# Rolling 28 of 32 batch tiles of a pairwise-product kernel into a staged hardware loop

## The chip, the cores and the metric

The kernel runs on one core of a Trainium2 chip. The metric is the device time of one execution in microseconds (us).

## The reference, cut to what matters

```python
# inputs: x (4096, 32, 64) float32, W (496, 64, 64) float32
i_idx, j_idx = np.triu_indices(32, k=1)            # 496 pairs i < j
vdotw = jnp.einsum('bpd,pde->bpe', x[:, i_idx, :], W)
return (vdotw * x[:, j_idx, :]).reshape(4096, -1)  # (4096, 31744)
```

Each row has 32 fields of 64 numbers. For every pair of fields, the first is multiplied by a matrix of that pair and the product, element by element, by the second field. The output has 520 MB, against 42 MB of input and weights that are read.

## The kernel before

The 4096 rows are cut into 32 batch tiles of 128 rows. The weights stay in SBUF. For each tile the kernel loads x (1 MB, issued by ScalarE's queue), transposes it with TensorE (PE in the profile), multiplies it with the weights of two fields at a time into one of four PSUM slots, and VectorE (DVE) multiplies the slot with x into a slice of a ring in SBUF. Five stores per tile, of 7552, 6528, 5504, 6336 and 5824 columns, carry the slices to the output. SyncE (SP in the profile) issues them. Engines wait for each other and for transfers: in the profile of this kernel SyncE waits 159 times for DVE before a store, and DVE 53 times for a store to land. All 32 tiles are unrolled.

```python
STORES = [[0, 1], [2, 3], [4, 5], [6, 7, 8], [9, 10, 11, 12, 13, 14, 15]]
RING = 28160
...
xpool  = ctx.enter_context(tc.tile_pool(name="x", bufs=2))
xtpool = ctx.enter_context(tc.tile_pool(name="xT", bufs=2))
psum   = ctx.enter_context(tc.tile_pool(name="ps", bufs=4, space=bass.MemoryType.PSUM))
...
ring = const.tile([P, RING], F32, tag="ring", name="ring")
...
for t in range(NT):                                   # 32 tiles, unrolled
    xt, xT = xs.pop(t), xTs.pop(t)
    if t + 1 < NT:
        xs[t + 1] = load_x(t + 1)                     # next x, one tile ahead
    for s, group in enumerate(STORES):
        if at + store_w[s] > RING:
            at = 0
        osb = ring[:, at : at + store_w[s]]
        at += store_w[s]
        for p in group:
            ...                                       # transposes of the next tile
            nc.tensor.matmul(pm[...], xT[...], w_sb[p][...])
            nc.vector.tensor_tensor(osb[...], pm[...], xt[...], ALU.mult)
        nc.sync.dma_start(out=out[ts(t, P), o0 : o0 + store_w[s]], in_=osb)
```

Of the kernel before, what the change touches and what calls it, by code (L numbers as in the profile page):

```python
# [1 line left out]

# [6 lines left out]

F32 = mybir.dt.float32  # L10
ALU = mybir.AluOpType

P = 128
BANK = 512

STORES = [[0, 1], [2, 3], [4, 5], [6, 7, 8], [9, 10, 11, 12, 13, 14, 15]]
PREFETCH_AT = [5, 6]
RING = 28160


@with_exitstack
def pair_bilinear_kernel(
    ctx: ExitStack,
    tc: tile.TileContext,
    x: bass.AP,
    w: bass.AP,
    out: bass.AP,
    F: int,
    D: int,
):  # L30
















    nc = tc.nc
    B = x.shape[0]
    NT = B // P
    NPR = F // 2  # L50

    width = [(F - 1 - i) * D for i in range(F)]
    off = [sum(width[:i]) for i in range(F)]
    woff = [sum(width[0 : 2 * p : 2]) for p in range(NPR)]
    store_w = [sum(width[2 * p] + width[2 * p + 1] for p in g) for g in STORES]

    const = ctx.enter_context(tc.tile_pool(name="const", bufs=1))
    xpool = ctx.enter_context(tc.tile_pool(name="x", bufs=2))
    xtpool = ctx.enter_context(tc.tile_pool(name="xT", bufs=2))
    psum = ctx.enter_context(tc.tile_pool(name="ps", bufs=4, space=bass.MemoryType.PSUM))  # L60

    ident = const.tile([P, P], F32, tag="ident", name="ident")
    make_identity(nc, ident)

    def runs(tl, a, b, n):

        ap = tl[:, a : a + n]
        return bass.AP(ap.tensor, ap.offset, [list(ap.ap[0]), [b - a, 2], list(ap.ap[1])])

    def load_x(t):  # L70
        xt = xpool.tile([P, F * D], F32, tag="x", name=f"x_{t}")
        nc.scalar.dma_start(out=xt, in_=x[ts(t, P), :])
        return xt

    def transpose_x(xT, t, xt, g):

        n = 2 * BANK // P
        pt = psum.tile([P, 2 * BANK], F32, tag="ps", name=f"pt_{t}_{g}")
        for c in range(n):
            nc.tensor.transpose(pt[:, ts(c, P)], xt[:, ts(n * g + c, P)], ident)  # L80
        nc.scalar.copy(xT[:, ts(g, 2 * BANK)], pt)  # L81

    def new_xT(t):
        return xtpool.tile([P, NPR * P], F32, tag="xT", name=f"xT_{t}")

    ring = const.tile([P, RING], F32, tag="ring", name="ring")
    at = 0
    xs = {0: load_x(0)}

    w_sb = []  # L90
    for p in range(NPR):
        wp = const.tile([P, width[2 * p]], F32, tag=f"w{p}", name=f"w{p}")
        nc.sync.dma_start(out=wp, in_=w[:, woff[p] : woff[p] + width[2 * p]])
        w_sb.append(wp)

    xTs = {0: new_xT(0)}
    for g in range(2):
        transpose_x(xTs[0], 0, xs[0], g)

    for t in range(NT):  # L100
        xt, xT = xs.pop(t), xTs.pop(t)
        if t + 1 < NT:
            xs[t + 1] = load_x(t + 1)
        for s, group in enumerate(STORES):
            if at + store_w[s] > RING:
                at = 0
            osb = ring[:, at : at + store_w[s]]
            at += store_w[s]
            o0 = off[2 * group[0]]
            for p in group:  # L110
                if t + 1 < NT and p in PREFETCH_AT:
                    if t + 1 not in xTs:
                        xTs[t + 1] = new_xT(t + 1)
                    transpose_x(xTs[t + 1], t + 1, xs[t + 1], PREFETCH_AT.index(p))
                for c0 in range(0, width[2 * p], BANK):
                    pm = psum.tile([P, 2, BANK], F32, tag="ps", name=f"pm_{t}_{p}_{c0}")
                    n = [max(0, min(BANK, width[2 * p + h] - c0)) for h in range(2)]
                    for h in range(2):
                        if n[h]:
                            nc.tensor.matmul(  # L120
                                pm[:, h, : n[h]],
                                xT[h * D : (h + 1) * D, ts(p, P)],
                                w_sb[p][h * D : (h + 1) * D, c0 : c0 + n[h]],
                                start=True,
                                stop=True,
                            )
                    o = [off[2 * p + h] - o0 + c0 for h in range(2)]
                    xj = [(2 * p + h + 1) * D + c0 for h in range(2)]
                    if n[0] == n[1]:
                        nc.vector.tensor_tensor(  # L130
                            runs(osb, o[0], o[1], n[0]),
                            pm[:, :, : n[0]],
                            runs(xt, xj[0], xj[1], n[0]),
                            ALU.mult,
                        )
                    else:
                        for h in range(2):
                            if n[h]:
                                nc.vector.tensor_tensor(  # L139
                                    osb[:, o[h] : o[h] + n[h]],  # L140
                                    pm[:, h, : n[h]],
                                    xt[:, xj[h] : xj[h] + n[h]],
                                    ALU.mult,
                                )
            nc.sync.dma_start(out=out[ts(t, P), o0 : o0 + store_w[s]], in_=osb)


# [33 lines left out]
```

## Time and profile before

| | before |
|---|---|
| time, median of 2 runs | 1341.47 us (1341.44 to 1341.51) |
| span of the profiled run | 1339.7 us |
| mean granted TensorE clock, as a share of full speed | 0.949 |
| DVE busy, PE busy | 88%, 86% of the span |
| a store from issue to landing | 22 us |
| one batch tile in the steady state, between landings of the last stores of neighbouring tiles | 41.0 to 41.3 us, some up to 41.7 |

The prediction below shows the lines of the page and of the waits that carry the reading. A second view places one tile in the middle of the kernel: busy time of each engine in a window that is one tile long. Its columns are the window and its length, the busy time of each engine with the number of instructions, the granted clock, the busy share of the DMA engines, and what they moved.

```profile
core 0: us, PE busy (x) PEld busy (x) DVE busy (x) ACT busy (x) POOL busy (x), PEclk, DMA share, GB/s
800.00:841.00 41.00, 34.37 (x162) 15.83 (x162) 35.27 (x50) 2.02 (x2) 0.00 (x0) 0.96 0.98 412
```

In 41 us DVE is busy for 35.3 us and PE for 34.4 us, while the DMA engines are busy 98% of the time. The transfers bound the tile. The next lines of the same page are the queues that fetch instructions.

```profile
q8 instruction: 42, 0.69, 0.2%
q14 instruction: 23, 0.19, 0.0%
```

### The profile page before, as it was taken

The page shows a single profiled execution, that of the slowest core. Times are in us where ns is not written, and L with a number is a line of the kernel's source. Part 1 is how long each engine was busy: PE and PEld are TensorE (multiplying, and loading weights), DVE is VectorE, ACT ScalarE, POOL GpSimd, SP SyncE. Part 2 cuts the span into 40 slices and gives each one's busy share as a digit, 9 for nine tenths or more (in the row PEclk, how much of TensorE's full clock was granted, in tenths as well). Part 3 has the DMA queues.
Part 4 walks back from the last instruction along what each step waited for, and adds up shares of the span by engine and source line. Part 5 has one row for each costly group of instructions (what it writes and reads, how often), then busy time and mean ns, then how long its engine had stood idle before and what let it go on. Part 6 is the DMA issues. An engine that isn't in the chain of part 4 may idle for free.

```text
span 1339.7 us, 13755 instructions
## 1 busy us (share of the span) xinstructions
PE 1151.0 (86%) x5376; PEld 548.7 (41%) x5376; DVE 1177.4 (88%) x1664; ACT 66.1 (5%) x65; POOL 0.7 (0%) x6
## 2 busy tenths in 40 slices
PE   7998889888898888988888978889798897888992
PEld 3444344443343443443433534444344443444441
DVE  6999889888899988989888989899898997898993
ACT  1000000000000000000000000000000000000000
POOL 0000000000000000000000000000000000000000
PEclk9999889999999999989999899899898998998996
DMA  9999999999999999999999999999999999999996
GB/s 392 426 431 434 429 431 429 427 427 434 426 434 430 422 422 430 422 424 429 415 426 424 426 426 404 415 420 431 428 420 408 431 427 431 416 424 420 422 429 264
DMA packets 30017, 562.93 MB, mean 420 GB/s; under 512 B 3456, under 2 KB 3840, under 8 KB 5376
## 3 DMA queue, kind: packets, MB, share of 16 engines
q1 hardware_dynamic: 25344, 528.49, 92.6%
q10 hardware_dynamic: 4608, 33.56, 6.0%
q8 instruction: 42, 0.69, 0.2%
q14 instruction: 23, 0.19, 0.0%
HBM read 41.94 MB, written 520.09 MB: 420 GB/s over the span
## 4 chain that ended last, share of the span: by engine, by line
DMA 54%; DVE 23%; PE 11%; issue 9%; DVEq 0%
DMA out_dram<-ring 54%; DVE ring L130 15%; PE pm L120 9%; DVE ring L139 9%; PE pt L80 2%; DMA x<-in_x_dram 1%; DVEq L130 0%; DVEq L177 0%
## 5 line engine op out<-in xcount | busy, mean ns | idle before, releaser
L120 PE MATMUL pm<-w,xT 64*128 64x512 f32 (+7 forms) x4864 | 1083.2, 559 | 158.3 <-DVE ring L130 140.1
L130 DVE TENSOR_TENSOR ring<-pm,x 128x1024 f32<-128x1024 f32 x768 | 904.0, 1217 | 138.4 <-DMA out_dram<-ring 93.0
L120 PEld LDWEIGHTS pm<-w,xT 64*128 64x128 f32 x4864 | 487.7, 194 | 720.1 <-DVE ring L130 451.3
L139 DVE TENSOR_TENSOR ring<-pm,x 128x448 f32<-128x448 f32 (+6 forms) x896 | 330.2, 415 | 3.6 <-PE pm L120 2.9
L81 ACT COPY xT<-pt 128x1024 f32<-128x1024 f32 x64 | 64.8, 1012 | 1194.6 <-PE pt L80 1194.6
L80 PE MATMUL pt<-ident,x 128*128 128x128 f32 x512 | 76.5, 297 | 8.5 <-DMA x<-in_x_dram 8.5
L80 PEld LDWEIGHTS pt<-ident,x 128*128 128x128 f32 x512 | 61.0, 152 | 48.9 <-issue 35.3
L81 ACT ACT_TABLE_LOAD x1 | 1.3, 1283 | 1.7 <-PEq L173 1.7
masks.py:199 POOL TENSOR_SCALAR_AFFINE_SELECT ident<-ident 128x128 f32<-128x128 f32 x1 | 0.3, 292 | 0.1
masks.py:197 POOL MEMSET ident<- 128x128 f32 x1 | 0.2, 204 | 0.3 <-POOLq L173 0.3
L173 POOL MEMSET const-bfloat16-1.0<- 128x1 bf16 x1 | 0.1, 101 | 0.0
L173 POOL MEMSET const-uint8-127<- 128x1 uint8 x1 | 0.1, 101 | 0.0
L173 POOL MEMSET const-float32-0.0<- 128x1 f32 x1 | 0.1, 98 | 0.2 <-issue 0.2
L173 POOL MEMSET const-float32-1.0<- 128x1 f32 x1 | 0.1, 98 | 0.0
## 6 DMA issues: line engine op xcount, KB each, us to landing
out_dram<-ring SPq DMA_DIRECT2D x32, 3776.0 KB, 22.8
out_dram<-ring SPq DMA_DIRECT2D x32, 3264.0 KB, 21.8
out_dram<-ring SPq DMA_DIRECT2D x32, 3168.0 KB, 22.4
out_dram<-ring SPq DMA_DIRECT2D x32, 2912.0 KB, 22.3
out_dram<-ring SPq DMA_DIRECT2D x32, 2752.0 KB, 22.1
x<-in_x_dram ACTq DMA_DIRECT2D x32, 1024.0 KB, 14.2
w<-in_w_dram SPq DMA_DIRECT2D x1, 992.0 KB, 7.4
w<-in_w_dram SPq DMA_DIRECT2D x1, 928.0 KB, 11.7
```

What stands on the lines that cost most here:

```text
L80: nc.tensor.transpose(pt[:, ts(c, P)], xt[:, ts(n * g + c, P)], ident)
L81: nc.scalar.copy(xT[:, ts(g, 2 * BANK)], pt)
L120: nc.tensor.matmul(pm[:, h, : n[h]], xT[h * D : (h + 1) * D, ts(p, P)], w_sb[p][h * D : (h + 1) * D, c0 : c0 + n[h]], start=True, stop=True,)
L130: nc.vector.tensor_tensor(runs(osb, o[0], o[1], n[0]), pm[:, :, : n[0]], runs(xt, xj[0], xj[1], n[0]), ALU.mult,)
L139: nc.vector.tensor_tensor(osb[:, o[h] : o[h] + n[h]], pm[:, h, : n[h]], xt[:, xj[h] : xj[h] + n[h]], ALU.mult,)
L173: nc = bacc.Bacc("TRN2", target_bir_lowering=False, num_devices=1)
```

## The change

The intent is a smaller program: two tiles stay unrolled at the head and two at the tail, and the 28 between them become seven iterations of a hardware loop whose body holds four tiles. In place of rotating pools, x, its transpose and the PSUM slots become fixed buffers, used in the same order as before. The loop is "staggered": its body is divided into four stages, one per tile, and the semaphores of a stage are reset when the engines have left it, so that engines need not all meet at the end of an iteration. The step from the end of one iteration to the start of the next is called the back edge here. The row address of every load and store inside the loop is a register plus a constant. The ring becomes 1888 columns smaller and starts at column 0 in every iteration.

```diff
-RING = 28160
+RING = 26272
+HEAD = 2
+BODY = 4
 ...
-    xpool = ctx.enter_context(tc.tile_pool(name="x", bufs=2))
-    xtpool = ctx.enter_context(tc.tile_pool(name="xT", bufs=2))
-    psum = ctx.enter_context(tc.tile_pool(name="ps", bufs=4, ...))
+    xbuf = [const.tile([P, F * D], F32, ...) for k in range(2)]
+    xTbuf = [const.tile([P, NPR * P], F32, ...) for k in range(2)]
+    slots = [pspool.tile([P, 2, BANK], F32, ...) for k in range(4)]
 ...
-            nc.sync.dma_start(out=out[ts(t, P), o0 : o0 + store_w[s]], in_=osb)
+            nc.sync.dma_start(out=out[bass.ds(row, P), o0 : o0 + store_w[s]], in_=osb)
+
+    for t in range(HEAD):
+        batch_tile(t * P, t % 2, (t + 1) * P)
+    turn["at"] = 0
+    tail = NT - (NT - HEAD - 1) % BODY - 1
+    with tc.For_i(HEAD * P, tail * P, BODY * P, iteration_sync="staggered") as r:
+        for j in range(BODY):
+            batch_tile(r + j * P, (HEAD + j) % 2, r + (j + 1) * P)
+            if j + 1 < BODY:
+                tc.stage_boundary()
+    turn["at"] = 0
+    for t in range(tail, NT):
+        batch_tile(t * P, t % 2, (t + 1) * P if t + 1 < NT else None)
```

`batch_tile(row, k, nxt)` is the body of the old loop, with `xbuf[k]` for x and `nxt` as the row of the next load.

More of the change, by code (lines that the diff above doesn't have):

```diff
@@ L57, in pair_bilinear_kernel, with slot @@
     const = ctx.enter_context(tc.tile_pool(name="const", bufs=1))
-    xpool = ctx.enter_context(tc.tile_pool(name="x", bufs=2))
-    xtpool = ctx.enter_context(tc.tile_pool(name="xT", bufs=2))
-    psum = ctx.enter_context(tc.tile_pool(name="ps", bufs=4, space=bass.MemoryType.PSUM))
+    pspool = ctx.enter_context(tc.tile_pool(name="ps", bufs=1, space=bass.MemoryType.PSUM))
     ident = const.tile([P, P], F32, tag="ident", name="ident")
     make_identity(nc, ident)
+    ring = const.tile([P, RING], F32, tag="ring", name="ring")
+    xbuf = [const.tile([P, F * D], F32, tag=f"x{k}", name=f"x{k}") for k in range(2)]
+    xTbuf = [const.tile([P, NPR * P], F32, tag=f"xT{k}", name=f"xT{k}") for k in range(2)]
+    slots = [
+        pspool.tile([P, 2, BANK], F32, tag=f"ps{k}", name=f"ps{k}") for k in range(4)
+    ]
+    turn = {"slot": 0, "at": 0}
+    def slot():
+        turn["slot"] = (turn["slot"] + 1) % 4
+        return slots[turn["slot"]]
     def runs(tl, a, b, n):
@@ L68, in runs, with load_x, transpose_x @@
         return bass.AP(ap.tensor, ap.offset, [list(ap.ap[0]), [b - a, 2], list(ap.ap[1])])
-    def load_x(t):
-        xt = xpool.tile([P, F * D], F32, tag="x", name=f"x_{t}")
-        nc.scalar.dma_start(out=xt, in_=x[ts(t, P), :])
-        return xt
-    def transpose_x(xT, t, xt, g):
+    def load_x(row, k):
+        nc.scalar.dma_start(out=xbuf[k], in_=x[bass.ds(row, P), :])
+    def transpose_x(k, g):
         n = 2 * BANK // P
-        pt = psum.tile([P, 2 * BANK], F32, tag="ps", name=f"pt_{t}_{g}")
+        pt = slot().rearrange("p a b -> p (a b)")
         for c in range(n):
-            nc.tensor.transpose(pt[:, ts(c, P)], xt[:, ts(n * g + c, P)], ident)
-        nc.scalar.copy(xT[:, ts(g, 2 * BANK)], pt)
-    def new_xT(t):
-        return xtpool.tile([P, NPR * P], F32, tag="xT", name=f"xT_{t}")
-    ring = const.tile([P, RING], F32, tag="ring", name="ring")
-    at = 0
-    xs = {0: load_x(0)}
+            nc.tensor.transpose(pt[:, ts(c, P)], xbuf[k][:, ts(n * g + c, P)], ident)
+        nc.scalar.copy(xTbuf[k][:, ts(g, 2 * BANK)], pt)
+    load_x(0, 0)
     w_sb = []
@@ L94, in pair_bilinear_kernel, with batch_tile @@
         w_sb.append(wp)
-    xTs = {0: new_xT(0)}
     for g in range(2):
-        transpose_x(xTs[0], 0, xs[0], g)
-    for t in range(NT):
-        xt, xT = xs.pop(t), xTs.pop(t)
-        if t + 1 < NT:
-            xs[t + 1] = load_x(t + 1)
+        transpose_x(0, g)
+    def batch_tile(row, k, nxt):
+        xt, xT = xbuf[k], xTbuf[k]
+        if nxt is not None:
+            load_x(nxt, 1 - k)
         for s, group in enumerate(STORES):
-            if at + store_w[s] > RING:
-                at = 0
-            osb = ring[:, at : at + store_w[s]]
-            at += store_w[s]
+            if turn["at"] + store_w[s] > RING:
+                turn["at"] = 0
+            osb = ring[:, turn["at"] : turn["at"] + store_w[s]]
+            turn["at"] += store_w[s]
             o0 = off[2 * group[0]]
             for p in group:
-                if t + 1 < NT and p in PREFETCH_AT:
-                    if t + 1 not in xTs:
-                        xTs[t + 1] = new_xT(t + 1)
-                    transpose_x(xTs[t + 1], t + 1, xs[t + 1], PREFETCH_AT.index(p))
+                if nxt is not None and p in PREFETCH_AT:
+                    transpose_x(1 - k, PREFETCH_AT.index(p))
                 for c0 in range(0, width[2 * p], BANK):
-                    pm = psum.tile([P, 2, BANK], F32, tag="ps", name=f"pm_{t}_{p}_{c0}")
+                    pm = slot()
                     n = [max(0, min(BANK, width[2 * p + h] - c0)) for h in range(2)]
@@ L144, in pair_bilinear_kernel @@
                                 )
-            nc.sync.dma_start(out=out[ts(t, P), o0 : o0 + store_w[s]], in_=osb)
+            nc.sync.dma_start(out=out[bass.ds(row, P), o0 : o0 + store_w[s]], in_=osb)
+    for t in range(HEAD):
+        batch_tile(t * P, t % 2, (t + 1) * P)
+    turn["at"] = 0
+    first_slot = turn["slot"]
+    tail = NT - (NT - HEAD - 1) % BODY - 1
[4 more added lines that the diff above has]
+                tc.stage_boundary()
+    assert turn["slot"] == first_slot
+    turn["at"] = 0
+    for t in range(tail, NT):
+        batch_tile(t * P, t % 2, (t + 1) * P if t + 1 < NT else None)
 def kernel(r_inputs, L0_rec_W):
```

## The prediction

> **What bounds the kernel now.** I read the page first, its slices, queues and chain, then the waits of the issuing queue, then the waits of the engines. The slices show whether anything rests:
>
> ```profile
> span 1339.7 us, 13755 instructions
> PE 1151.0 (86%) x5376; PEld 548.7 (41%) x5376; DVE 1177.4 (88%) x1664; ACT 66.1 (5%) x65; POOL 0.7 (0%) x6
> ...
> DMA  9999999999999999999999999999999999999996
> GB/s 392 426 431 434 429 431 429 427 427 434 426 434 430 422 422 430 422 424 429 415 426 424 426 426 404 415 420 431 428 420 408 431 427 431 416 424 420 422 429 264
> ...
> q1 hardware_dynamic: 25344, 528.49, 92.6%
> q10 hardware_dynamic: 4608, 33.56, 6.0%
> ...
> DMA 54%; DVE 23%; PE 11%; issue 9%; DVEq 0%
> ```
>
> The transfers never rest: the DMA row is 9 in every slice but the last, and the two data queues fill 98.6% of the 16 engines' time. The stores (q1) are most of it, and the chain that ended last is 54% store. PE and DVE are at 86% and 88%, so the kernel is transfer-bound, with DVE some 4 to 5 us per batch tile behind it (1339.7 less 1177.4, over 32 tiles).
>
> Why the transfers never rest is in the list of issues and in the waits of SyncE, which issues all stores:
>
> ```profile
> out_dram<-ring SPq DMA_DIRECT2D x32, 3776.0 KB, 22.8
> out_dram<-ring SPq DMA_DIRECT2D x32, 3264.0 KB, 21.8
> ...
> SPq L145 <- DVE ring L139: 1228.7, 159, 10.5
> ...
> DVE ring L130 <- DMA out_dram<-ring: 93.0, 53, 3.3
> ```
>
> A store takes 22 us from issue to landing, though one is issued about every 8.3 us (160 stores in 1330 us): two to three are always queued. SyncE waits 159 times, every time for DVE to have filled the slice of the ring and never for a store to land. DVE in its turn waits 93 us for old stores to free the ring. So each store's start-up and acknowledgement are hidden beneath the stores queued ahead of it. That is what I look at in the change.
>
> [...] packet records show one row of the 5824-column store (23,296 bytes) taking 865 ns, or 26.9 GB/s on each of 16 engines. The first weight load's first packet starts 1.0 us after its issue on an idle queue, and the last store lands 0.45 us after its last packet. No run yet shows a store alone. [...]
>
> **The change part by part.** Arithmetic, matmuls, multiplies, loads and stores are the same in number and shape. The smaller ring keeps the reuse distance: I walked both placements, and a slice still comes back after three or four stores. The fixed PSUM slots turn in the same order as the pool. What is new are waits, and I took them from the built program, instruction by instruction.
>
> 1. *Stores one after another.* In the loop the row address of a store is a register, and the program orders stores to the output against each other. The second store of a stage waits for the semaphore that the first one raises on landing, the third for the second, and so on; a stage's first store waits for the last one of the stage before. In the kernel before a store waits for DVE and for a semaphore last used about eight transfers earlier. So inside the loop exactly one store is in flight, and its fixed cost is exposed every time.
>  Cost of a store alone: eight rows per engine at 26.9 GB/s, which is 8.97, 7.76, 6.54, 7.53 and 6.92 us for the five, 37.7 us per tile. The fixed part: 1.0 us to the first packet, 0.45 us from last packet to landing, 0.1 us to wake SyncE[...]: 1.9 us[...]. Five of them: 9.5 us. The x load of the next tile (8192-byte packets, eight per engine at 309 ns, 2.5 us) now starts at the stage's entry and shares the engines with one store: 2.5 us. [...] A loop tile costs 37.7 + 9.5 + 2.5 + 0.5 = **50.2 us**, against 41.5 before (from the landings of equal stores in neighbouring tiles).
>
> 2. *Stage gates.* An engine enters a stage only when all have left the stage two back, and SyncE says so only at its own entry, after it has issued the last store of the stage just before. So PE cannot run ahead over a boundary: it starts the next tile when that last store is issued. From there 0.4 us of waits, 1.3 us for the first matmuls and 8.5 us of DVE work (spacing of stores in the unobstructed second tile) make the next tile's first store ready after 10.2 us. The last store lands after 6.9 + 2.5 + 1.9 = 11.3 us. The gate is therefore just hidden by the serial store, and I charge nothing; 1.1 us is little slack.
>
> 3. *The back edge.* In the first stage of an iteration DVE's very first multiply, too, waits for all five stores of the iteration's end to land. The 8.5 us of DVE work then lie bare, with 0.2 us of semaphores: **8.7 us** for each of six back edges, 52 us. [...]
>
> 4. *Entry and exit.* Two head tiles run as before; their stores would land by 110.6 us after the start. DVE may finish the loop's first slice only after the last of them: the first loop store is issued near 115.5 us. The last two tiles run unserialised again. From the issue of the loop's last store I count 12 us until the next can start, two tiles of transfers (75.4 + 2.5 us) and 1.5 us for start and landing: 91 us.
>
> Sum: 115.5 + 28 x 50.2 + 52 - 11.3 (the last store's own time, counted in the tail) + 91 = 1653 us, and 1.8 us for the time over the span (1341.5 against 1339.7): **1655 us**.
>
> **Rivals.**
> - *Hidden anyway.* If the waits on landing were already met when reached, DVE being late, nothing would change: 1340 to 1360 us. Against it: DVE needs 38 us per tile unobstructed and the serial stores 47 us, so DVE is always ahead, and the wait is on the transfer just issued, which cannot have landed.
> - *Gates alone.* If I misread the store semaphores and only the stage gates counted, each boundary would cost DVE about 2 us of start-up, against 4 to 5 us of slack per tile: within 2%, with entry and exit perhaps 1365 us. For it: the list of the kernel before names the same family of semaphores, harmlessly. Against it: in the loop the store's semaphore is the one raised by its predecessor.
> - [...]
> - *Less than I count.* If the fixed cost of a store is 1.5 us, the 140 stores give back 56 us: 1600 us.
>
> **Range and chances.** The fixed cost is the term that matters: 0.1 us of it is 14 us of time. From 1.5 to 2.4 us[...] I get 1590 to 1730 us. Only the first two rivals bring it below a 2% loss (1368 us), and the built program speaks against both: slower by over 2% with 0.97, within 2% with 0.025, faster with 0.005. There is no way to be faster that I see: the bytes stay.
>
> **What would show it.** Step 1 is right if SyncE's waits move from DVE to its own stores in the loop, if a store takes 8.5 to 13 us to landing instead of 22, and if the DMA row falls to 8. Step 2 is right if the first slice of a tile is ready about when the last store lands; wrong if SyncE waits for DVE at each boundary. Step 3 is right if seven regular pauses of some 9 us stand in the transfers, about 210 us apart. DVE's and PE's busy sums should stay near 1177 and 1151 us, a longer PE sum meaning a lower clock. The prediction is wrong if stores still overlap in the loop, or if a lone store's fixed cost is outside 1.5 to 2.4 us.

The packet records are those of the kernel before. The fixed part of a store came to 1.9 us: the three terms make 1.55 us, and the rest was an allowance. The loop tile came to 50.2 us, and its 0.5 us are such an allowance too. So the 1655 us hold about 28 x (5 x 0.35 + 0.5) = 63 us that rest on no trace. A rival that put more time at the boundaries and the back edges is cut; without it the range from 1.5 to 2.4 us is 1599 to 1725 us. The small terms that stay are estimates from the profile of before: 0.1, 0.2 and 0.4 us of waking and waiting (there, DVE multiplies 0.12 us after a landing, 1278.88 to 1279.00 us), and 1.3 us for the first matmuls (1.18 us from the first matmul, at 11.98 us, to the first multiply).

## The result and the profile after

| | before | after |
|---|---|---|
| time, median of 2 runs | 1341.47 us | 1630.63 us (1630.26 to 1631.0) |
| ratio, 95% interval | | 1.2156 (1.2103 to 1.2208) |
| span, mean granted clock | 1339.7 us, 0.949 | 1629.2 us, 0.873 |
| one batch tile | 41.0 to 41.3 us | 48.9 to 49.8 us, and 56.0 to 56.3 us with a back edge |

A ratio here is the mean time of one kernel's runs over that of the other's of the same rounds, so it is not quite the ratio of the medians that are quoted. The kernel became 289 us slower. The page of the kernel after:

```profile
span 1629.2 us, 14956 instructions
PE 1175.0 (72%) x5376; PEld 558.4 (34%) x5376; DVE 1175.1 (72%) x1664; ACT 66.1 (4%) x65; POOL 0.7 (0%) x6
...
PEclk9977988789887898888988899888998889988798
DMA  9987787788887888877888778887788877888799
...
q1 hardware_dynamic: 25344, 528.49, 77.6%
q10 hardware_dynamic: 4608, 33.56, 4.9%
q8 instruction: 10, 0.16, 0.0%
q14 instruction: 7, 0.06, 0.0%
...
out_dram<-ring SPq DMA_DIRECT2D x32, 3776.0 KB, 10.3
out_dram<-ring SPq DMA_DIRECT2D x32, 3264.0 KB, 9.2
```

The work is unchanged: the same counts of matmuls and multiplies, DVE's busy sum 1175.1 us as against 1177.4, and the same number of packets on the two data queues. PE's busy sum is 1175.0 us as against 1151.0, at a mean granted clock of 0.873 as against 0.949. But no engine is close to full any more. The stores and loads fill 82.5% of the DMA engines' time instead of 98.6%, and the row of slices is 7 or 8 wherever the loop runs and 9 in the unrolled ends. A store takes 10.3 us from issue to landing where it took 22.8: nothing is queued ahead of it. The waits of SyncE name the reason; the columns are the total, the number of waits and the longest.

```profile
SPq L149 <- DMA out_dram<-ring: 1029.5, 118, 11.8
SPq L149 <- DVE ring L143: 453.2, 78, 19.0
```

Before, 159 waits of stores were for DVE and none for another store. Now 118 are for a store to land. The other 78 are for DVE (one store can have both waits); the long ones among them, as the windows and the timelines below show, are at the boundaries of tiles.

Three windows that each hold one tile of the loop, from the first store of a tile to that of the next; the first holds a back edge, and the third ends 0.7 us later than its tile (columns as before):

```profile
270.04:326.27 56.23, 37.26 (x166) 17.80 (x166) 36.58 (x53) 2.02 (x2) 0.00 (x0) 0.85 0.74 308
326.27:375.86 49.59, 37.06 (x174) 17.99 (x172) 36.91 (x53) 2.02 (x2) 0.00 (x0) 0.86 0.84 349
375.86:425.50 49.64, 36.59 (x174) 17.20 (x172) 37.40 (x53) 2.02 (x2) 0.00 (x0) 0.90 0.83 349
```

DVE still needs only 37 us of each tile. The inner tile in the second window has 49.6 us, in which DMA is busy 83 to 84%. I took one such tile apart with the packet records, in which the profile gives start and length of every DMA packet. From the landing of one store, SyncE issues the next after 0.12 us; the first packet starts 0.83 us after the issue; the 16 engines end within 0.15 us of each other; the landing is signalled 0.37 us after the last packet. That is 1.47 us in every store in which the engines move nothing. The medians from issue to landing are 10.34, 9.17, 7.92, 8.90 and 10.51 us. The fifth shares the engines with the load of x and takes 2.2 us longer than without it. The five add up to 46.8 us, four wakings of 0.12 us make it 47.3, and the rest of the 49.6 us is a gap before a tile's first store.

That gap is the second thing to see. The timeline at the boundary of two tiles (start, duration, engine, operation; idle time before it in brackets). The last store of the old tile was issued at 363.11 and landed at 373.65; the first of the new one was issued at 375.86:

```profile
363.95 12.54 PE L124 MATMUL ps<-w,xT 64*128 64x512 f32 x48 [10.95 <-issue]
364.93 0.37 PEld L124 LDWEIGHTS ps<-w,xT 64*128 64x128 f32 x2 [0.48 <-issue]
365.79 0.37 PEld L124 LDWEIGHTS ps<-w,xT 64*128 64x128 f32 x2 [0.49 <-issue]
366.17 1.22 DVE L134 TENSOR_TENSOR ring<-ps,x 128x1024 f32<-128x1024 f32 x1 [11.54 <-PE ps L124]
...
371.01 0.28 PEld L124 LDWEIGHTS ps<-w,xT 64*128 64x128 f32 x2 [0.15 <-issue]
371.44 0.28 PEld L124 LDWEIGHTS ps<-w,xT 64*128 64x128 f32 x2 [0.15 <-issue]
```

PE has been idle for 10.95 us: the stage gate holds it until SyncE has issued the old tile's last store. It then starts slowly. Its pairs of weight loads come 0.86 us apart, and from 369.1 on 0.43 us apart, twice as fast. The granted clock of these two stretches, the column after POOL, is half and full:

```profile
363.11:368.92 5.81, 4.97 (x12) 2.37 (x14) 2.30 (x2) 0.00 (x0) 0.00 (x0) 0.50 0.88 342
368.92:375.86 6.94, 6.94 (x34) 3.40 (x32) 6.64 (x10) 0.00 (x0) 0.00 (x0) 1.00 0.75 295
```

DVE starts 3.06 us after the store's issue, and its slice is ready 12.75 us after it, when the store has already been down for 2.2 us.

The third is the back edge. The last store of the iteration landed at 317.26:

```profile
317.38 3.48 DVE L134 TENSOR_TENSOR ring<-ps,x 128x1024 f32<-128x1024 f32 x3 [19.10 <-DMA out_dram<-ring]
...
326.27 0.34 SPq L149 DMA_DIRECT2D out_dram<-ring  x1
```

DVE waited for the transfers to end and then filled a whole slice while nothing moved: 9.0 us. All six back edges have it, between 8.75 and 9.02 us.

### The profile page after: what moved, and what is told of

The parts are those of the page before. It is cut to its first block, busy times and chain, and to the rows that moved or that the text cites. A ratio compares the mean times of both kernels' runs of the same rounds, so it can differ in the third digit from the quotient of the medians.

```text
span 1629.2 us, 14956 instructions
## 1 busy us (share of the span) xinstructions
PE 1175.0 (72%) x5376; PEld 558.4 (34%) x5376; DVE 1175.1 (72%) x1664; ACT 66.1 (4%) x65; POOL 0.7 (0%) x6
## 5 line engine op out<-in xcount | busy, mean ns | idle before, releaser
L124 PE MATMUL ps<-w,xT 64*128 64x512 f32 (+7 forms) x4864 | 1112.3, 574 | 429.5 <-issue 305.1
L134 DVE TENSOR_TENSOR ring<-ps,x 128x1024 f32<-128x1024 f32 x768 | 904.1, 1213 | 439.7 <-PE ps L124 307.4
L124 PEld LDWEIGHTS ps<-w,xT 64*128 64x128 f32 x4864 | 502.0, 199 | 1012.7 <-issue 523.0
L143 DVE TENSOR_TENSOR ring<-ps,x 128x448 f32<-128x448 f32 (+6 forms) x896 | 327.5, 411 | 0.0
L92 ACT COPY xT<-ps 128x1024 f32<-128x1024 f32 x64 | 64.8, 1012 | 1495.9 <-PE ps L91 1495.9
L91 PE MATMUL ps<-ident,x 128*128 128x128 f32 x512 | 71.4, 284 | 8.6 <-DMA x<-in_x_dram 8.6
L91 PEld LDWEIGHTS ps<-ident,x 128*128 128x128 f32 x512 | 56.4, 143 | 42.0 <-issue 42.0
## 6 DMA issues: line engine op xcount, KB each, us to landing
out_dram<-ring SPq DMA_DIRECT2D x32, 3776.0 KB, 10.3
out_dram<-ring SPq DMA_DIRECT2D x32, 2912.0 KB, 10.5
```

The source lines that it names most:

```text
L91: nc.tensor.transpose(pt[:, ts(c, P)], xbuf[k][:, ts(n * g + c, P)], ident)
L92: nc.scalar.copy(xTbuf[k][:, ts(g, 2 * BANK)], pt)
L124: nc.tensor.matmul(pm[:, h, : n[h]], xT[h * D : (h + 1) * D, ts(p, P)], w_sb[p][h * D : (h + 1) * D, c0 : c0 + n[h]], start=True, stop=True,)
L134: nc.vector.tensor_tensor(runs(osb, o[0], o[1], n[0]), pm[:, :, : n[0]], runs(xt, xj[0], xj[1], n[0]), ALU.mult,)
L143: nc.vector.tensor_tensor(osb[:, o[h] : o[h] + n[h]], pm[:, h, : n[h]], xt[:, xj[h] : xj[h] + n[h]], ALU.mult,)
```

## The experiments

The theory has three parts: stores that wait for their predecessor (**order**), stage gates that start a tile too late (**gates**), and a multiply that waits for a whole stage of stores (**back edge**). The rivals are that one of them alone carries the time, or that the loop itself (branches, fetches, registers) costs it. All kernels below gave the reference's result. The kernel before ran beside each group with medians of 1341.21, 1341.44 and 1341.24 us.

### e4_serial: the order alone, without a loop

The kernel before, unrolled, with one wait added from each store to the previous one.

```diff
-            nc.sync.dma_start(out=out[ts(t, P), o0 : o0 + store_w[s]], in_=osb)
+            st = nc.sync.dma_start(out=out[ts(t, P), o0 : o0 + store_w[s]], in_=osb)
+            if last:
+                tc.add_manual_dep(st.ins, last.pop().ins.name, SYNC, reason="one store at a time")
+            last.append(st)
```

> The unrolled kernel of before with one thing added: each store waits until the store before it has landed; no loop, no stages, no branch. Theory (store order): a tile costs what a tile of the changed kernel costs without its stage gap, 49.6 - 2.2 = 47.4 us, so 24.5 us until the first store, 32 x 47.4 us, and 1.8 us: 1543 us, range 1525 to 1560. Rival (the loop's machinery, that is gates, semaphore resets, branch and instruction fetch, costs most): nothing of it is here, so about 1341 us, at most 1400.

Measured: **1621.75 us** (2 runs), ratio 1.2092 (1.2049 to 1.2135). The waits and the slices:

```profile
SPq L147 <- DMA out_dram<-ring: 1524.7, 159, 13.6
...
DMA  9888888888888889888887888878888888878888
```

Order alone, with no loop, no gate and no back edge, costs 280 us. That confirms the mechanism, but it is 79 us more than I expected, so the expectation missed. The packet records point to a reason. This unrolled program fetches instructions in 65 packets, as before does. Of 140 stores in tiles 2 to 29, 55 had a fetch in flight, and these took 1.0 to 1.4 us longer on average than the same store without one (the first of a tile 11.35 us against 10.35). That is some 66 us, if the fetch is what makes the difference. In the kernel before the 65 fetch packets lie under queued stores, which take 22 us from issue to landing. e10_serial_loop below repeats the serial stores without the fetches.

### e1_nodep: the order taken away, the loop kept

```diff
+            st = nc.sync.dma_start(out=out[bass.ds(row, P), o0 : o0 + store_w[s]], in_=osb)
+            tc.add_to_no_dep_group("stores", st.ins)
+            tc.declare_no_dep(st.ins, group="stores", reason="rows and columns are disjoint")
```

> The changed kernel with the stores declared independent of each other inside an iteration; gates, resets, back edge and branch stay. Theory: the serial part goes, the 6 back edges (DVE still waits for the last store of an iteration) cost some 10 us of idle transfers each and the entry 5 us, the gates take about 3 us of DVE time per boundary, which its slack of some 3 us nearly covers: 1410 us, range 1375 to 1445. Rival (loop machinery): hardly less than 1630, at least 1550.

Measured: **1408.46 us** (2 runs), ratio 1.0502 (1.0471 to 1.0532).

```profile
SPq L149 <- DVE ring L143: 1161.6, 159, 19.1
SPq L149 <- DMA out_dram<-ring: 93.9, 12, 8.7
...
DMA  9998999879998899978999789997999969999998
```

Three quarters of the loss are gone (222 of 289 us), SyncE waits for DVE again, and the DMA row is 9 but for a dip at every fifth slice. Inner tiles take 41.3 us, as before, with the gates still there. The tiles after a back edge take 50.9 us, 9.8 us more; six of them and 5.6 us at the entry of the loop make 64 of the 67 us that remain over before. So the loop as such costs nothing in an inner tile, and the gates cost nothing while stores are queued.

### e2_early: the gates opened earlier, the order kept

Each engine announces that it has left the previous stage after the second store of its tile instead of at its entry to the next stage.

```diff
+            if early and s == 1:
+                for e in LEAVE:                 # SP, DVE, PE, Activation
+                    tc.previous_stage_wait(e)
```

> The changed kernel with SyncE, DVE, PE and ScalarE signing out of the stage before already after the second store of a stage, so that PE may cross the next boundary without waiting for the last store to be issued; stores still one after another. Theory: the gap before a tile's first store falls from 2.2 us (1.2 to 2.4) to 0.1 us at 21 inner boundaries, 44 us in all; the back edge keeps its 9 us: 1587 us, range 1575 to 1600. Rival (loop machinery is most of the 289 us): below 1450.

Measured: **1596.39 us** (2 runs), ratio 1.1903 (1.1868 to 1.1938), 34.2 us less than after.

```profile
SPq L151 <- DMA out_dram<-ring: 1232.7, 139, 11.3
SPq L151 <- DVE ring L145: 208.8, 45, 19.0
```

The gap before a tile's first store is 0.02 us at all 21 inner boundaries and still 8.76 to 9.02 us at the six back edges. SyncE's waits for DVE fall from 453 to 209 us. 34.2 us over 21 boundaries is 1.6 us each, a little less than the gaps that vanished (most of them 1.7 to 2.4 us). The load of x is issued at another point and now mostly shares the engines with the third store instead of the fifth. By the stores' times to landing it costs 2.7 us a tile on average there, against 2.2 to 2.3 us in the kernel after. That is some 13 us over the loop, and it accounts for the 10 us between the 44 us of gaps that vanished and the 34 us that were won.

### e7_halves: the back edge, by two rings

The ring becomes two buffers of 14080 columns with two stores in each, so that the first multiply of an iteration meets a buffer whose last store is the third of the stage before, not the fifth.

```diff
-RING = 26272
+RING = 14080
-    ring = const.tile([P, RING], F32, tag="ring", name="ring")
+    ring = [const.tile([P, RING], F32, tag=f"ring{k}", name=f"ring{k}") for k in range(2)]
...
+            at = turn["at"] if turn["n"] % 2 else 0
+            osb = ring[turn["n"] // 2 % 2][:, at : at + store_w[s]]
+            turn["n"], turn["at"] = turn["n"] + 1, at + store_w[s]
```

> The changed kernel with the ring made of two buffers of 14080 columns, two stores in each, so that DVE's first multiply of an iteration waits only for the stores of its own half, which landed long before. Reuse distance 4 everywhere. Theory: the gap at the 6 back edges falls from 9.0 us to the 2.3 us of an inner boundary, 40 us: 1590 us, range 1578 to 1605. Rival (the back edge gap is the branch and its instruction fetch): 1630 us, unchanged.

Measured: **1584.14 us** (2 runs), ratio 1.1812 (1.1777 to 1.1846), 46.5 us less than after. The gap at a back edge falls from 9.0 us to between 1.7 and 2.15 us, which is the gap of the inner boundaries. Six times 6.9 us is 41 us. The rest is the same wait at the loop's entry, where the ring's restart makes DVE wait for the head's stores: the first store of the second loop tile is issued at 160.2 us instead of 167.0. The end of the kernel gives 1.7 us of it back. The slices lose their regular sevens:

```profile
DMA  9998787888888888888888888888888888888799
```

Since the branch is still there and the gap at a back edge is now like that at an inner boundary, no cost of the branch is left to be seen.

### e8_nodep_early: order and gates removed

The edits of e1 and e2 together.

> The changed kernel with the stores declared independent and the early signing-out together; only the back edge is left. In the run with independent stores alone the inner tiles already took 41.3 us against 41.1 before and those at the back edge 50.9. Theory: early signing-out gives at most 0.2 us at 21 boundaries, and the 6 back edges keep 9.8 us each: 1404 us, range 1390 to 1412. Rival (the gates hold back the transfers although the inner tiles look untouched): under 1380.

Measured: **1409.06 us** (4 runs), ratio 1.0506 (1.0488 to 1.0523). It is the time of e1. Inner tiles take 40.8 to 41.4 us and those after a back edge 51.2 to 51.5. Opening the gates is worth 34 us when stores are serial and nothing when they are queued.

### e9_all: all three removed

The edits of e1, e2 and e7.

> The changed kernel with all three: independent stores, early signing-out, and the ring in two halves so that DVE does not wait for the last store at the back edge. SyncE still waits there for the last store to land. Theory: 6 back edges x 1.5 us of fixed cost are all that is left, 1341 + 9 = 1350 us,[...] 1343 us, range 1325 to 1360. Rival (a loop costs something more that these three do not cover): above 1370.

Measured: **1355.01 us** (4 runs), ratio 1.0100 (1.0083 to 1.0117).

```profile
DMA  9999999989999899999999899998999989999998
...
SPq L150 <- DVE ring L144: 975.5, 141, 12.2
SPq L150 <- DMA out_dram<-ring: 126.2, 18, 9.8
```

This accounts for all but 13.5 us of the 289. Inner tiles take 41.1 to 41.3 us, as before. The six tiles after a back edge take 42.7 us, 1.5 us more: there SyncE still waits for a landing, and the fixed cost of one store lies bare. That is 9 us. Of the other 4 us, 1 us lies outside the profiled span (2.9 us of time over the span instead of 1.8), and the rest is spread over head and inner tiles. I had expected 1343 us, 12 us too low though inside the range given: 1350 us with the wait at the back edge, less 7 us from a term that no run had shown. The loop's fewer fetches (17 packets instead of 65) give nothing back where stores are queued.

### c1_before_halves: the two rings without a loop

A control: the kernel before with the two half rings of e7.

> Control: the unrolled kernel of before with its ring made of the same two halves; no loop. If a gain of the run with all three came from the ring, it is here too. Theory: the same capacity, so 1341 us, range 1334 to 1347.

Measured: **1341.76 us** (4 runs), ratio 1.0002 (0.9986 to 1.0019). The half rings are neutral on their own, so what they win in e7 and e9 is the wait at the back edge.

### e5_barrier: no stages, a barrier at each iteration's end

```diff
-    with tc.For_i(HEAD * P, tail * P, BODY * P, iteration_sync="staggered") as r:
+    with tc.For_i(HEAD * P, tail * P, BODY * P, iteration_sync="barrier") as r:
...
-            if j + 1 < BODY:
-                tc.stage_boundary()
```

> The changed kernel with the loop's semaphores reset at a full barrier between iterations in place of the stages; stores still one after another. Theory: the 2.2 us gaps at the inner boundaries go (3 per iteration), and the gap at the back edge grows from 9 us[...] to some 13 us: 7 x 2.6 us less, 1612 us, range 1590 to 1640. Rival (a barrier and its resets are dear): above 1660.

Measured: **1611.43 us** (4 runs), ratio 1.2009 (1.1989 to 1.2029).

```profile
DMA  9988788688886888868888688886888868888699
```

There is a 6 at every fifth slice, a pause of 12.4 to 12.6 us at each back edge (the 13 us expected were an estimate), and gaps of only 0.11 to 0.13 us inside an iteration. The sums give most of a reason for the 19 us by which it beats the staggered loop: 6 x 12.5 + 21 x 0.1 = 77 us of gaps, against 6 x 9.0 + 21 x 2.2 = 100 us, while the pause at the loop's exit is longer, 12.9 us against 4.2. With serial stores, resetting in stages, which was to save the meeting of all engines, cost more here than the meeting.

### e10_serial_loop: the serial stores by themselves, in the loop

The edits of e2 and e7, with the order kept.

> The changed kernel with the early signing-out and the two ring halves, the stores still one after another: gates and back edge gone, so it does what the unrolled kernel with serial stores (1621.8 us) does, but as a loop that fetches its instructions once. Theory: gaps and serial stores add up, 1584 us of the run with halves less 28 x 1.6 us, 1540 us, range 1525 to 1555; and the 80 us to the unrolled serial kernel are its 48 more instruction fetches, each of which falls on a lone store (stores with a fetch in flight took 1.0 to 1.4 us longer there), and the place of the x load. Rival (the loop and the unrolled form cost the same once stores are serial): about 1620 us.

Measured: **1539.15 us** (4 runs, 1536.64 to 1540.85), ratio 1.1475 (1.1456 to 1.1494).

```profile
SPq L150 <- DMA out_dram<-ring: 1238.5, 139, 17.6
SPq L150 <- DVE ring L144: 148.5, 34, 12.6
...
DMA  9997888888888888888888888888888888888799
```

Gates and back edges gone, 198 us over before remain. The order is 184 us of them, since e9 differs from this kernel in the order alone and takes 1355.01 us: 6.6 us for each of the 28 loop tiles (a tile takes 47.9 us on average here). The other 14 us are what is left in e9 too. The time is 83 us less than e4. Some 27 us of that are the four tiles at the ends, which are not serial here (4 times 48.0 less 41.2), which my expectation had overlooked. The other 56 us are of the size of the fetches counted in e4 (66 us), which no run isolates. In the kernel after, no fetch packet is recorded between 245 and 1526 us.

### e11_split: twice as many serial stores

e10 with every store cut into two of half the columns.

```diff
+            hw = store_w[s] // 2
+            for a in (0, hw):
+                nc.sync.dma_start(
+                    out=out[bass.ds(row, P), o0 + a : o0 + a + hw], in_=osb[:, a : a + hw]
+                )
```

> The same kernel with every store split into two of half the columns: 10 serial stores per tile in place of 5, the bytes and all else unchanged. It measures the fixed cost by itself. Theory: 0.12 us to wake SyncE, 0.83 to the first packet, 0.15 of spread and 0.37 to landing are 1.47 us, times 140 more stores, 206 us: 1746 us, range 1725 to 1775. Rival (the serial stores are slow because a lone store moves its bytes more slowly, not because of a fixed cost): at most 1580 us.

Measured: **1756.64 us** (4 runs), ratio 1.3087 (1.3065 to 1.3109).

```profile
SPq L152 <- DMA out_dram<-ring: 1365.0, 279, 9.1
...
DMA  9977777777777777777777777777777777777799
```

The bytes are the same and 140 serial stores are added. (1756.64 - 1539.15) / 140 = **1.55 us** for each, which confirms the 1.47 us read from the packets in the kernel after. The rival is out: without 1.35 us of fixed cost after its issue, the first store of a tile takes 8.99 us for its bytes, as the prediction had it from the rate of before (8.97).

## Why the prediction was right

The predicted 1655 us stand against 1630.63, inside the range. The waits of all four steps were found as described; what failed is the verdict of step 2 that the gate is hidden. This is the ledger, with the parts taken away one after another:

| part | from | us |
|---|---|---|
| back edges, and the entry | after less e7 | 46.5 |
| gates | e7 less e10 | 45 |
| order of the stores | e10 less e9 | 184 |
| what stays in the loop | e9 less before | 13.5 |
| sum | | 289 |

The sum is right by construction, and the parts depend on the order of removal. With the order of the stores taken away first they are 222 us for it (e1), nothing for the gates (e8), 54 us for the back edges (e8 less e9) and the same rest.

The parts were not equally well sized, and that the sum came so close is partly luck. Step 1 is too dear by 2.9 us a tile, 81 us in all, and step 2 leaves out 45 us. With step 1 sized right and the gates still free, the prediction would have been about 1574 us, below its range.

**Step 1, the order of the stores: right, too dear.** SyncE's waits moved to its own stores, the stores take 7.9 to 10.5 us and the DMA row is 7 to 8. The fixed cost was 1.47 us by packets and 1.55 us by e11, and not 1.9. The rival "Less than I count" had named 1.5 us, which the prediction also gave as the limit below which it would be wrong: the two readings lie on either side of it. The first packet came after 0.83 us instead of 1.0, the landing 0.37 us after the last packet instead of 0.45, and the 16 engines end within 0.15 us of each other, where the allowance comes to 0.35 by the sum. Five stores: 2.1 us a tile too much. The load of x took 2.2 us instead of 2.5. The further 0.5 us, the allowance for instruction fetches, was not seen after the first iteration: no fetch packet is recorded between 245 and 1526 us. The 41.5 us for a tile of before, given for comparison only, should have been 41.1.

**Step 2, the gates: wrong.** "Just hidden, and I charge nothing" is the step that failed. The gate itself is as described, but the slice was ready 12.75 us after the release, not 10.2, while the store landed after 10.54 us, not 11.3. The bare gap is 1.2 to 2.4 us at inner boundaries, and e7 to e10 price the gates at 45 us. DVE started 3.1 us after the release where I counted 1.7, behind a PE whose granted clock was 0.50 in its first five us (363.95 to 368.92). The record of the clock in this trace has 0.50 from 355.3 us, inside PE's pause of 10.95 us, to 368.9. In the kernel before it has that after shorter pauses too: PE is idle from 142.6 to 146.0 us (its ends are modelled), and the clock is 0.50 from 145.0 to 151.8. An estimate from the trace of after: of the 2.5 us by which the slice is later, 0.9 us lie in the first matmuls (2.2 us instead of 1.3) and 0.75 us in DVE's two waits for PE, all at half clock. The other 0.9 us are 0.4 us more until PE starts and 0.4 us more of DVE work. At full clock the gap would then have been about 0.5 us. No run kept PE at full clock through the gate, so this share is not tested.

Steps 1 and 2 together: 50.2 - 2.1 - 0.3 - 0.5 + 2.2 = 49.5 us, and inner tiles took 48.9 to 49.8.

**Step 3, the back edge: right.** 9.0 us bare, against 8.7. But the gap takes the place of the 2.2 us of an inner boundary, so a tile there takes 6.6 us more than another. There are six such pauses; the seventh that the prediction looked for is the entry, where the bare gap was 3.2 us. No branch cost showed (e7), and no fetch packet is recorded in the six back edges.

**Step 4, entry and exit: right.** The first loop store was issued at 114.2 us (predicted 115.5), and from the issue of the last one to the last landing it took 92.7 us (91). That a slice comes back after three or four stores does not hold at the entry: the ring restarts there, and the first slice comes back after one store. Step 4 has the wait that follows from it.

Thus the whole error lies in the loop: from its first store to the issue of its last it took 1421.4 us, and the prediction has 28 x 50.2 + 52 - 11.3 = 1446.3.

**The rivals.** "Hidden anyway" and "gates alone" both fall: e4 shows that the order alone costs 280 us in an unrolled program (some 66 us of it with its fetches), and e8 that the gates cost nothing once stores overlap. "A loop costs by itself" falls with e9, whose inner tiles take what they took before.

No kernel tried here beats the one before. The best loop, e9, is 1.0% behind it.

**Left open.** The share of the half clock in the gates' 45 us; what a fetch costs a lone store, which only e4's averages show; and in the kernel before the tile of 41.1 us itself, which is about 1 us more than the prediction's 37.7 + 2.5 us of packets.

## What to carry to other kernels

When a loop gives stores an address that the program can't compare, look at what each store waits for: if it is the landing of the one before, every store shows its fixed cost (here about 1.5 us, 184 us in all between e10 and e9), and saying that the stores are disjoint wins it back. A stage boundary cost nothing here as long as transfers were queued across it (e1 against e8, 1408.46 and 1409.06 us), and left gaps of 1.2 to 2.4 us where they were not, so remove the order first and the gates afterwards, and give a ring used across a back edge more than one buffer. A term that comes out "just hidden" by 1 us should be entered with half its possible size, not with zero.
